# Position products of layer 0 from a table of distances, gathered through memory, in a two-layer attention kernel

## The chip, the cores and the metric

The kernel runs on one core of a Trainium2 chip. TensorE (PE) multiplies matrices into PSUM[...]; VectorE (DVE) and ScalarE (ACT) read PSUM and work in SBUF; GpSimd (POOL) and SyncE (SP) issue transfers here. The metric is the device time of one execution in microseconds. The kernel before takes 3813.87 us (median of three runs, 3813.14 to 3814.92).

## The reference

Two layers of attention over images of 32 x 32 tokens, 4 images, 768 channels, 12 heads of 64. Each layer adds its result to its input, after a group norm:

```python
x = x + _L0_conv_ref(_gn(x), ...)
x = x + _L1_conv_ref(_gn(x), ...)
```

Both layers add to the scores a bias of relative positions, computed from the query itself. For layer 0:

```python
attn = jnp.einsum('bqd,bkd->bqk', q, k) / np.sqrt(HD)
Rh = _get_rel_pos(h, h, rel_h)
Rw = _get_rel_pos(w, w, rel_w)
rel_bias_h = jnp.einsum('bhwc,hkc->bhwk', rq, Rh)
rel_bias_w = jnp.einsum('bhwc,wkc->bhwk', rq, Rw)
attn = attn.reshape(b * NH, h, w, h, w) + rel_bias_h[:, :, :, :, None] + rel_bias_w[:, :, :, None, :]
```

`Rh[h, k]` is row `h - k + 31` of a table of 63 rows: only the distance counts. So a query in image row h meets 32 neighbouring rows of the table, a window that moves with h; and the same for columns. Layer 1 does the same after a 3 x 3 depthwise convolution and a layer norm of q, k and v.

## The kernel before

**Pairs and stages.** Two heads are worked together as a pair: 64 channels each on 128 partitions. A stage is one image in one layer, six pairs (hp 0 to 5). The eight stages run in the order image 0 and 1 in layer 0, then both in layer 1, then images 2 and 3 likewise: 48 pairs, of which 0 to 11 and 24 to 35 are layer 0. While pair i is attended, pair i + 1 is prepared.

**Attention (`attend`).** For each of two chunks c of 512 queries and each of two groups g of four key blocks, PE computes four score blocks: two heads' q.k products (L820) and two products of the bias with a 0/1 matrix (L822). ACT takes the exponentials (L827). DVE sums them in layer 0 (L836, L838). PE multiplies with the values (L844, av). The sums of the last chunk are finished with a product z (L789) and four ACT instructions.

**Steps.** The loop yields four times for each group, twice behind the scores and twice behind av, so a pair has 16 steps. Scores are written just ahead of steps 0, 4, 8 and 12, av just ahead of 2, 6, 10 and 14. `Pair.plan` gives each piece of the preparation a step; `at` collects the pieces of a step in a list, and they are emitted in that order into each engine's queue. There is no scheduler: an engine works its queue strictly in order. Within a step, pieces of the group norm, of `mix_tokens` (L303) and of `mix_weights` (L290, L291) were put in the list ahead of those of the pairs, projections behind them.

**Layer 0 preparation.** Pair 0 and 1 compute q, k and v plainly. From pair 2 on (`in_sevens`), two pairs' products are made together by seven block products instead of eight (`sevens`): Q in two pieces at steps 0 and 2 (which make q and k of the pair), V at steps 8 and 10 for even hp only. So pairs with odd hp have few pieces. Pair 24 (`shift`) has all 4 steps later. For q, ACT writes the tile q and also q_t, the same with rows and columns exchanged (L495, L496).

**Position products (`positions`).** In two halves of 16 image rows and columns, PE multiplies for each row and head a 32-row window of the table with 32 queries: 64 products of 64 x 32 by 32 a half (L613), all into one bank. ACT copies them to the tile whole (L618 contiguous, L619 strided). In layer 0 pairs of the sevens the halves are at steps 6 and 8 (8 and 10 for pair 24).

**`split`** (step 10, or 12 for pair 24) casts whole to a rounded copy, high (L629, ACT), leaves the rest in whole (L630, DVE), and POOL issues the transfers that spread both into the two bias tiles (L640): 16 a pair, 8 for each chunk.

**PSUM.** Two banks are the first score tile's (ps_a), one av's, one small. The other four are two places, `place_b` and `place_c`, two banks each. A place is opened anew for each user: the second score block of each group takes both banks of place_b, the third both of place_c, and between them the preparation's products take singles of them. A new user waits until the old one has been read. The fourth score block uses ps_a again and waits for the first block's exponential.

**Transfers.** SP issues loads and stores in its own order; an issue that waits holds up those behind it. Weights are loaded two uses ahead.

## Time and profile before

| | |
|---|---|
| median of three runs | 3813.87 us |
| the profiled execution | 3816.61 us |
| its span, first to last instruction | 3814.6 us |
| granted TensorE clock | 0.997 |
| position products in PE, L613 | 123.6 + 122.7 us busy, both layers |
| q_t, L496 (ACT) | 48 + 22 + 22 + 4 instructions, 1.14 to 1.28 us |
| copies of positions, L618 and L619 (ACT) | 96 each, 54.9 and 99.9 us |
| cast to high, L629 (ACT) | 48, 49.9 us |
| rest in whole, L630 (DVE) | 48, 58.5 us |
| bias transfers, L640 (POOL) | 768, 2.9 and 3.0 us to landing |

A row of the groups names line, engine, operation, output and inputs, shape, count; then the time busy and the mean duration in ns; then the idle time of the engine ahead of it and what ended it. On PE each float32 product stands as two instructions, and successive products overlap, so a mean duration is longer than a product's share of the time; what a product costs is read from the starts in the timeline. A timeline row gives the start in us, the length of the merged row, engine, line, operation, tiles, shapes, count, and in brackets the idle time ahead of it with its releaser. From one start of scores to the next, a layer 0 pair with odd hp takes 55 us where nothing else is put beside it, and one with even hp some 74 us.

### The profile page before, as it was taken

The page shows a single profiled execution, that of the slowest core. Times are in us where ns is not written, and L with a number is a line of the kernel's source. Part 1 is how long each engine was busy: PE and PEld are TensorE (multiplying, and loading weights), DVE is VectorE, ACT ScalarE, POOL GpSimd, SP SyncE. Part 2 cuts the span into 40 slices and gives each one's busy share as a digit, 9 for nine tenths or more (in the row PEclk, how much of TensorE's full clock was granted, in tenths as well). Part 3 has the DMA queues.
Part 4 walks back from the last instruction along what each step waited for, and adds up shares of the span by engine and source line. Part 5 has one row for each costly group of instructions (what it writes and reads, how often), then busy time and mean ns, then how long its engine had stood idle before and what let it go on. Part 6 is the DMA issues. An engine that isn't in the chain of part 4 may idle for free. (4 is left out here: it accounts for less than half of the span.)

```text
span 3814.6 us, 76313 instructions
## 1 busy us (share of the span) xinstructions
PE 3749.5 (98%) x32990; PEld 1656.7 (43%) x32990; DVE 2467.1 (65%) x3068; ACT 1786.5 (47%) x2573; POOL 529.1 (14%) x964
## 2 busy tenths in 40 slices
PE   8999999999999999999999999999999999999998
PEld 4535535533344443444535445355343444434442
DVE  2566554559678877688454554445686888867874
ACT  2455434545355553455534544254442555525562
POOL 0111100111111211111200010001111112111120
PEclk9999999999999999999999999999999999999999
DMA  4344443331431223311333132523114212142123
GB/s 152 102 122 116 134 144 90 101 81 40 119 102 48 57 59 95 123 48 48 82 111 121 53 78 63 171 61 78 46 46 131 87 50 66 47 122 65 48 58 100
DMA packets 214024, 330.44 MB, mean 87 GB/s; under 512 B 50390, under 2 KB 103698, under 8 KB 213680
## 3 DMA queue, kind: packets, MB, share of 16 engines
q1 hardware_dynamic: 122912, 211.86, 17.9%
q0 software_dynamic: 90768, 113.61, 12.6%
q8 instruction: 263, 4.31, 0.5%
q14 instruction: 81, 0.66, 0.1%
HBM read 184.23 MB, written 40.10 MB: 59 GB/s over the span
## 5 line engine op out<-in xcount | busy, mean ns | idle before, releaser
L827 ACT ACTIVATE e<-s 128x1024 f32<-128x1024 f32 x768 | 775.6, 1024 | 423.7 <-PE s L822 393.6
L131 PE MATMUL qkv<-xn,wqkv_t 128*64 128x512 f32 x3648 | 816.0, 596 | 7.0 <-DVE gmean L334 2.6
L820 PE MATMUL s<-q,k 64*128 64x512 f32 x3072 | 808.7, 603 | 6.6 <-ACT e L827 3.1
L544 DVE SCALAR_TENSOR_TENSOR shared<-shared,sm 128x1056 f32<-128x1056 f32 x576 | 757.9, 1316 | 15.7
L822 PE MATMUL s<-bias,ones 64*128 64x512 f32 x1536 | 611.7, 790 | 1.1 <-DMA bias<-whole 1.0
L844 PE MATMUL av<-e,vt 128*64 128x512 f32 x2624 | 596.2, 596 | 0.0
L131 PEld LDWEIGHTS qkv<-xn,wqkv_t 128*64 128x64 f32 x3648 | 256.5, 137 | 484.0 <-issue 466.1
L640 POOL DMA_DIRECT2D bias<-high x384 | 205.6, 556 | 1794.6 <-ACT high L629 1559.7
L838 DVE TENSOR_TENSOR acc<-acc,e 128x1024 f32<-128x1024 f32 x294 | 360.0, 1225 | 114.0 <-ACT e L827 87.4
L820 PEld LDWEIGHTS s<-q,k 64*128 64x128 f32 x3072 | 279.5, 186 | 264.4 <-issue 213.3
L527 ACT ACTIVATE shared<-qkv,sm 128x512 f32<-128x512 f32 (+1 forms) x288 | 129.3, 502 | 469.7 <-PE qkv L131 469.7
L844 PEld LDWEIGHTS av<-e,vt 128*64 128x64 f32 x2624 | 185.4, 137 | 350.9 <-issue 316.8
L822 PEld LDWEIGHTS s<-bias,ones 64*128 64x128 f32 x1536 | 148.6, 187 | 185.4 <-issue 184.1
L640 POOL DMA_DIRECT2D bias<-whole x384 | 207.2, 571 | 53.2 <-DVE whole L630 46.3
L836 DVE TENSOR_TENSOR acc<-e 128x1024 f32<-128x1024 f32 x49 | 60.0, 1225 | 215.4 <-ACT e L827 206.8
L742 ACT COPY weighed<-av 128x512 f32<-128x512 f32 x96 | 56.3, 587 | 279.0 <-PE av L844 270.1
L559 DVE TENSOR_REDUCE mean<-ln_c 128x8 f32<-128x512 f32 x144 | 98.6, 685 | 106.0 <-PE ln_c L556 106.0
L771 POOL DMA_DIRECT2D weighed<-last x94 | 50.7, 541 | 679.6 <-ACT last L768 638.6
L613 PEld LDWEIGHTS rel<-q,rel 64*32 64x32 f32 x6144 | 112.1, 106 | 68.6 <-issue 63.8
L613 PE MATMUL rel<-q_t,rel 64*32 64x32 f32 x6144 | 123.6, 195 | 1.8 <-issue 1.8
L613 PE MATMUL rel<-q,rel 64*32 64x32 f32 x6144 | 122.7, 195 | 1.9 <-issue 1.9
L412 DVE TENSOR_TENSOR shared<-shared,m3m 128x512 f32<-128x512 f32 x66 | 45.3, 687 | 119.9 <-PE m3m L131 119.8
(162 smaller groups left out, 4439.0 us busy)
## 6 DMA issues: line engine op xcount, KB each, us to landing
bias<-high POOLq DMA_DIRECT2D x384, 128.0 KB, 2.9
bias<-whole POOLq DMA_DIRECT2D x384, 128.0 KB, 3.0
wqkv_t<-in_wqkv SPq DMA_DIRECT2D x78, 384.0 KB, 3.2
wqkv_t<-mixed SPq DMA_DIRECT2D x66, 384.0 KB, 3.1
wproj_t<-mixed SPq DMA_DIRECT2D x48, 384.0 KB, 3.3
wqkv_t<-in_wqkv SPq DMA_DIRECT2D x66, 192.0 KB, 2.5
xn<-in_x SPq DMA_DIRECT2D x24, 512.0 KB, 7.7
x<-in_x SPq DMA_DIRECT2D x48, 256.0 KB, 3.2
```

What stands on the lines that cost most here:

```text
L131: nc.tensor.matmul(ps[lo : lo + D], a[:, lo : lo + D], b, start=start, stop=stop, **kw)
L527: nc.scalar.activation(self.pad[s][:, rows, there : there + src.shape[2]], src, AF.Identity, bias=col(self.column(s)))
L544: nc.vector.scalar_tensor_tensor(y, window, tap, y, ALU.mult, ALU.add)
L559: nc.vector.tensor_reduce(of, heads, AX.X, ALU.add)
L613: nc.tensor.matmul(ps[lo : lo + S, k * S : (k + 1) * S].rearrange("p (b c) -> p b c", b=2), rel[rows, 2 * self.layer + i, first : first + ...
L640: nc.gpsimd.dma_start(sets, some.unsqueeze(1).to_broadcast([D // 2, 2, QC]))
L820: nc.tensor.matmul(ps[:, j, :], k[rows, keys], q[rows, cols], start=True, stop=False)
L822: nc.tensor.matmul(ps[:, j, :], ones[rows, kt % 2 * P : (kt % 2 + 1) * P], bias[c][rows, kt // 2, :], start=False, stop=True,)
L827: nc.scalar.activation(e, ps, AF.Exp)
L836: nc.vector.tensor_tensor(acc, es[0], es[1], ALU.add)
L838: nc.vector.tensor_tensor(acc, acc, e, ALU.add)
L844: nc.tensor.matmul(av[j * D : (j + 1) * D, :], pair.vt[:, kt, j * D : (j + 1) * D], e[:, j, :], start=(kt == 0), stop=(kt == NKT - 1),)
```

## The change

Pairs 1 to 11 and 24 to 35 no longer use `positions`. A block of queries that spans 16 image rows and 16 columns needs 47 neighbouring rows of the table, for all its queries together. `all_positions` multiplies all 64 channels with such a table: a stationary matrix of 64 x 128 holds 47 distances for rows and 47 for columns, for each combination of row half and column half (four in all). A call takes half of the queries, in two products of 256 queries for each head. The first head's result goes to one bank (rel0), read by ACT, the second's to another (rel1), read by DVE. Each is copied in two parts, one contiguous in runs of 16 and one strided, to tiles that take the buffers of q_t and whole.

Each query's result is now 47 distances from which 32 are wanted, at an offset that depends on its row or column. `keep_positions` stores both heads' results to memory (two stores of 512 KB), and `call_positions` reads them back with eight transfers, in which each image row (or column) starts one partition's row further on: runs of 64 elements, 256 bytes. `split` then reads them from the tile raw in four ACT copies and four DVE subtractions of 64 x 512 instead of one of each.

The calls are at steps 3 (in place_c) and 4 (in place_b), store and gather at 6, split at the head of step 9 (pair 24: 7, 8, 10, and the head of 12). Halves of steps place a piece at the head of its step's list. q_t is made only where `positions` is still used: pair 0 and layer 1. The table's rows are no longer reversed, so windows, the 0/1 matrix (picks) and split's row choice are reversed to match; their cost is unchanged. The table is loaded once at the start.

```diff
+            self.by_table = not self.layer and self.i > 0
+            self.all = []
...
-                self.q_t = one.tile([P, T], F32, tag="q_t", name="q_t")
+                if not self.by_table:
+                    self.q_t = one.tile([P, T], F32, tag="q_t", name="q_t")
             nc.scalar.activation(self.q[:, cols], ps, AF.Identity, bias=bias, scale=scale)
+            if self.by_table:
+                return
...
+        def all_positions(self, b, place):
+            if not self.all:
+                self.all = [one.tile([P, T], F32, tag=tag, name="all_" + tag) for tag in ("q_t", "whole")]
+            place.n = 0
+            ps = [place.single(f"rel{j}") for j in range(2)]
+            for a in range(2):
+                tokens = slice(b * HALF + a * (HALF // 2), b * HALF + (a + 1) * (HALF // 2))
+                there = slice(a * (HALF // 2), (a + 1) * (HALF // 2))
+                for j in range(2):
+                    rows = slice(j * D, (j + 1) * D)
+                    nc.tensor.matmul(
+                        ps[j][:, there], table[rows, 2 * a + b, :], self.q[rows, tokens], start=True, stop=True
+                    )
+            for j, (to, copy) in enumerate(zip(self.all, (nc.scalar.copy, nc.vector.tensor_copy))):
+                copy(by_rows(to[:D], b), ps[j][:D].rearrange("p (s m c) -> p s m c", s=2, m=S // 2))
+                copy(by_columns(to[D:])[:, b], ps[j][D:].rearrange("p (a c) -> p a c", a=S))
+            if place is place_b:
+                other_work((place_c, place_c, place_b, place_b))
+
+        def keep_positions(self):
+            self.kept = dram.tile([P, 2, T], F32, tag="kept", name="kept", bufs=2)
+            for j, x in enumerate(self.all):
+                nc.sync.dma_start(self.kept[:, j, :], x)
+
+        def call_positions(self):
+            self.raw = one.tile([P, T], F32, tag="q_t", name="raw")
+            kept = self.kept[:, :, :]
+            step = 2 * T
+            for i in range(2):
+                for j in range(2):
+                    for h in range(2):
+                        first = i * D + j * S + h
+                        nc.sync.dma_start(
+                            self.raw[first : first + S - 1 : 2, :].rearrange("p (m x) -> p m x", m=S // 2),
+                            bass.AP(
+                                kept.tensor, kept.offset + (i * D + h * (S // 2)) * step + j * T,
+                                [[step, S // 2], [step + 2 * S, S // 2], [1, 2 * S]],
+                            ),
+                        )
...
-            nc.scalar.copy(high, self.whole)
-            nc.vector.tensor_tensor(self.whole, self.whole, high.bitcast(F32), ALU.subtract)
+            if self.by_table:
+                self.whole = one.tile([P, T], F32, tag="whole", name="low")
+                for b in range(2):
+                    cols = slice(b * HALF, (b + 1) * HALF)
+                    views = [
+                        (x[:D, cols].rearrange("p (s m c) -> p s m c", s=2, m=S // 2) for x in (high, self.whole)),
+                        (x[D:, cols].rearrange("p (a c) -> p a c", a=S) for x in (high, self.whole)),
+                    ]
+                    for (to, left), x in zip(views, (by_rows(self.raw[:D], b), by_columns(self.raw[D:])[:, b])):
+                        nc.scalar.copy(to, x)
+                        nc.vector.tensor_tensor(left, x, to.bitcast(F32), ALU.subtract)
+            else:
+                nc.scalar.copy(high, self.whole)
+                nc.vector.tensor_tensor(self.whole, self.whole, high.bitcast(F32), ALU.subtract)
...
-                first = 4 if shift(self.i) else 6
                 pieces += [
-                    (first, lambda: self.positions(0)),
-                    (first + 2, lambda: self.positions(1)),
-                    (first + 4, lambda: self.split()),
+                    (3, lambda: self.all_positions(1, place_c)),
+                    (4, lambda: self.all_positions(0, place_b)),
+                    (6, lambda: self.keep_positions()),
+                    (6, lambda: self.call_positions()),
+                    (8.5 if shift(self.i) else 9.5, lambda: self.split()),
                 ]
...
-        events.setdefault(step, []).append(piece)
+        events.setdefault(int(step), []).insert(0 if step % 1 else len(events.get(int(step), [])), piece)
...
+    at(-8, lambda: [nc.sync.dma_start(table[rows], tables[0]) for rows in (slice(0, D), slice(D, P))])
```

More of the change, by code (lines that the diff above doesn't have):

```diff
@@ L45, in two_layers @@
 @with_exitstack
-def two_layers(ctx: ExitStack, tc: tile.TileContext, keep, x_in, wqkv, wproj, rels, windows, vrow, small, const, onehot, picks, out):
+def two_layers(ctx: ExitStack, tc: tile.TileContext, keep, x_in, wqkv, wproj, rels, windows, tables, vrow, small, const, onehot, picks, out):
     nc = tc.nc
@@ L131, in halves, with by_rows, by_columns @@
             nc.tensor.matmul(ps[lo : lo + D], a[:, lo : lo + D], b, start=start, stop=stop, **kw)
+    def by_rows(x, b):
+        return x.rearrange("p (m s b c) -> p b s m c", m=S // 2, s=2, b=2)[:, b]
+    def by_columns(x):
+        return x.rearrange("p (c b a) -> p b a c", b=2, a=S)
     def image(x):
@@ L371, in two_layers @@
     seen = fixed.tile([P, 2 * len(items) * (T // QC)], F32, tag="seen", name="seen")
+    table = fixed.tile([P, 4, P], F32, tag="table", name="table")
     tiny = fixed.tile([P, 1], F32, tag="tiny", name="tiny")
@@ L611, in positions @@
                         lo = i * D + j * S
-                        first = 2 * (S - 1 - at)
+                        first = 2 * at
                         nc.tensor.matmul(
@@ L638, in split @@
                             sets = bias[2 + part :: 4, 2 * h : 2 * h + 2, :] if i else bias[part::4, h::2, :]
-                            some = src[i * D + h : (i + 1) * D : 2, cols]
+                            some = src[i * D + 1 - h : (i + 1) * D : 2, cols]
                             nc.gpsimd.dma_start(sets, some.unsqueeze(1).to_broadcast([D // 2, 2, QC]))
@@ L649, in plan @@
                     (2, lambda: self.plain(Q, 1)),
-                    (4, lambda: self.plain(K, 0)),
+                ] + ([
+                    (3, lambda: self.all_positions(0, place_c)),
+                    (4, lambda: self.all_positions(1, place_b)),
+                    (6, lambda: self.keep_positions()),
+                    (6, lambda: self.call_positions()),
+                    (9, lambda: self.split()),
+                ] if self.by_table else [
                     (5, lambda: self.positions(0)),
-                    (6, lambda: self.plain(K, 1)),
                     (7, lambda: self.positions(1)),
                     (8, lambda: self.split()),
+                ]) + [
+                    (4, lambda: self.plain(K, 0)),
+                    (6, lambda: self.plain(K, 1)),
                     (8, lambda: self.plain_v(0)),
@@ L662, in plan @@
                 ]
-                first = 4 if shift(self.i) else 6
                 pieces += [
-                    (first, lambda: self.positions(0)),
-                    (first + 2, lambda: self.positions(1)),
-                    (first + 4, lambda: self.split()),
+                    (3, lambda: self.all_positions(1, place_c)),
+                    (4, lambda: self.all_positions(0, place_b)),
+                    (6, lambda: self.keep_positions()),
+                    (6, lambda: self.call_positions()),
+                    (8.5 if shift(self.i) else 9.5, lambda: self.split()),
                 ]
@@ L1073, in general @@
 @with_exitstack
-def general(ctx: ExitStack, tc: tile.TileContext, bad, x_in, wqkv, wproj, rels, windows, vrow, small, const, onehot, picks, out):
+def general(ctx: ExitStack, tc: tile.TileContext, bad, x_in, wqkv, wproj, rels, windows, tables, vrow, small, const, onehot, picks, out):
     nc = tc.nc
@@ L1328, in _laid_out @@
     onehot = np.concatenate([np.arange(S)[:, None] == key // S, np.arange(S)[:, None] == key % S])
-    windows = np.stack([rels[..., h : h + 3 * S // 2 - 1] for h in (0, S // 2)], axis=-1)
+    rows = rels[..., ::-1]
+    windows = np.stack([rows[..., h : h + 3 * S // 2 - 1] for h in (0, S // 2)], axis=-1)
+    tables = np.zeros((2, D, 2, 2, 2, D), np.float32)
+    for i in range(2):
+        for half in range(2):
+            some = rows[i::2, :, half * (S // 2) : half * (S // 2) + 3 * S // 2 - 1]
+            which = (half, slice(None), 0) if i == 0 else (slice(None), half, 1)
+            tables[(slice(None), slice(None)) + which + (slice(0, some.shape[-1]),)] = some[:, :, None]
     picks = np.zeros((S // 2, 2, 2, 2, 2, 2, 8, S // 2), np.float32)
@@ L1334, in _laid_out @@
         for u in range(2):
-            picks[i, 0, :, :, :, u] = (8 * u + np.arange(8) == i)[:, None]
-        picks[i, 1, ..., i] = 1.0
+            picks[i, 0, :, :, :, u] = (8 * u + np.arange(8) == S // 2 - 1 - i)[:, None]
+        picks[i, 1, ..., S // 2 - 1 - i] = 1.0
     return {
@@ L1342, in _laid_out @@
         "windows": np.ascontiguousarray(windows.reshape(4, D, 3 * S - 2)),
+        "tables": np.ascontiguousarray(tables.reshape(2, D, 4, P)),
         "vrow": np.ascontiguousarray(f["L0_conv_bv"].reshape(1, C)),
```

## The prediction

> **What bounds the kernel now.** I read the page's busy shares first, then the groups of lines, then the timeline of one pair of layer 0, engine by engine.

> ```profile
> span 3814.6 us, 76313 instructions
> PE 3749.5 (98%) x32990; PEld 1656.7 (43%) x32990; DVE 2467.1 (65%) x3068; ACT 1786.5 (47%) x2573; POOL 529.1 (14%) x964
> ...
> L827 ACT ACTIVATE e<-s 128x1024 f32<-128x1024 f32 x768 | 775.6, 1024 | 423.7 <-PE s L822 393.6
> ...
> L618 ACT COPY whole<-rel 64x512 f32<-64x512 f32 x96 | 54.9, 572 | 28.3 <-PE rel L613 28.3
> ```

> TensorE is busy for 98%, so PE work removed is time won, and any wait put before PE is time lost: there are only 65 us of idle PE to hide in. The other two engines have room on average, but ACT waits for scores and PE for the exponentials' banks, so order counts. Pair 27, prepared while pair 26 is attended (2087.7 to 2142.9 us), on PE:

> ```profile
> 2119.27 3.65 PE L844 MATMUL av<-e,vt 128*64 128x512 f32 x16
> 2122.86 0.21 PE L613 MATMUL rel<-q,rel 64*32 64x32 f32 x1
> ...
> 2124.08 1.13 PE L820 MATMUL s<-q,k 64*128 64x512 f32 x4
> ...
> 2128.63 1.08 PE L789 MATMUL z<-acc,cst 128*64 128x512 f32 x4
> ...
> 2130.86 3.65 PE L844 MATMUL av<-e,vt 128*64 128x512 f32 x16
> 2134.44 1.13 PE L820 MATMUL s<-q,k 64*128 64x512 f32 x4
> ```

> Position products take 2122.86 to 2124.08, 1.22 us, and again between z and av: z to av is 2.23 us, of which z alone is 0.91 (2092.25 to 2093.16 earlier), leaving 1.3. And ACT there, then DVE in the attention of pair 4:

> ```profile
> 2129.75 0.60 ACT L790 ACTIVATE t<-z 128x512 f32<-128x512 f32 x1
> ...
> 2133.53 1.04 ACT L629 CAST high<-whole 128x1024 fp32r<-128x1024 f32 x1
> 2135.84 4.29 ACT L827 ACTIVATE e<-s 128x1024 f32<-128x1024 f32 x4 [1.26 <-PE s L822]
> ```

> ```profile
> 355.31 5.21 DVE L838 TENSOR_TENSOR acc<-acc,e 128x1024 f32<-128x1024 f32 x4 [1.70 <-ACT e L827]
> 360.44 1.75 DVE L303 TENSOR_TENSOR shared<-xn 128x1536 f32<-128x1536 f32 x1
> ```

> ACT has just 1.26 us of slack between the split's cast and the next exponentials. On DVE the token mixing runs at once behind the sums of exponentials.

> [...] two heads' q.k products plus two bias products take 1.09 us a block (2125.27 to 2126.36 on the same view), which 512-column passes of 0.43 us allow only if both heads overlap. [...] for ACT writes: L619, strided, 1041 ns against L618's 572. For DVE, and for strided reads, it shows nothing. [...]

> **The change, part by part.** A pass of 512 columns is 2.58/6 = 0.43 us (m4m, 12 instructions in two column groups, 2093.16 to 2095.74). Position products removed: 1.22 + 1.3 = 2.5 us a pair. Added: per call two halves of 256 columns, two passes each, heads side by side: 4 x 0.215 = 0.86, 1.72 a pair. [...] PE gain 0.8 us a pair, 23 pairs: **-18.4**.

> ACT loses q_t (2 x 1.17) and four L618/L619 copies (3.2) and one cast (1.04), and gains four rel0 copies (3.2) and four split copies (3.2): even, but elsewhere. DVE gains four copies from PSUM (0.69 each by L559's row) and four subtractions of 64x512 for one of 128x1024 (1.22): +4.3 us a pair, hidden by idle time except as below.

> *Third score block.* The first call, after the second sevens, holds place_c until ACT has copied rel0. ACT's k copy ends 2116.28; two copies 0.58 + 1.04 make 2117.9. PE, after 0.86 more and two blocks of 1.09, comes at 2117.86. With signal latency a wait of 0.15, 22 pairs: **+3.3**. Behind it the exponentials start 1.7 us later; they still end before av needs them.

> *Late DVE copies.* Where another piece stands ahead of rel1's copies on DVE, the score block that wants their bank waits. Pairs 5 and 29 (mix_tokens' pieces come first in step 4): sums of e end 2124.1 on pair 27's clock, then 2 x 1.75, then 2 x 0.69: 2129.0, against PE at 2125.9: 3.1 each. Pairs 6 and 10 (weight mixing, 5 x 0.55 us, ahead in step 3): rel1 at 2119.7 against 2117.9: 1.8 each. Together **+9.8**.

> *The round trip.* On pair 27's clock rel1's copies end at 2125.6. Two stores of 512 KB follow: the 256 KB store mid<-x lands in 3.1 us, and another 256 KB takes 0.7 to 0.9, so 3.9: 2129.6. SP then issues eight gathers. wproj_t<-in_wproj (384 runs of 512 B) takes 0.38 to issue, so about 0.45 apart: the eighth at 2132.9; landing like a 192 KB load's 2.3: 2135.2. Everything on SP behind these waits too, but the next weight loads are half a pair away. ACT cannot go past its first split copy: of the four (0.58, 1.04, 0.58, 1.04) the second needs the last gathers, so they end at 2137.9 and the next exponential at 2138.9. (Strided reads are not in the trace: 0.58 to 1.04 a copy; I take the strided write's 1.04, and at 0.58 the stall is 0.9 shorter.) PE has by then run av and three score blocks and wants that bank at 2137.3 (its clock, less 0.8): **1.8 to 2 us of stall**. Behind ACT here stand the exponentials, behind those av; the bias DMAs on POOL also start later, but land at about 2143.5, before the next pair's bias product at about 2144.7.

> Pairs with an even hp have V's first sevens (10.5 us of PE) at step 8, pairs 7, 25 and 31 a projection, 11 and 35 padded products: covered. Pair 1 is covered by plain K and V, pair 24 by V. Exposed: 3, 5, 9, 27, 29, 33 (the four of 55.2 us or so from start to start, and the like). Pairs 9, 27, 33: 2.0 each, **+6**. Pairs 5, 29: 1.8 each more, **+3.6**. Pair 3: weight mixing at step 6 has five stores ahead on SP, behind DVE's statistics (2.46) and mixing (2.66): the stores of positions start 5.8 us later: **+8**. Were the cover of the even pairs gone, each would pay the same 2 us.

> *Removed waits.* Two waits of next pair's bias (1.0 and 0.4 us) go, since the split's program place is earlier: **-1.4**. The table's load (two DMAs) is at the start, long before use: nothing. The picks and reversed rows change data only.

> Sum: -18.4 + 3.3 + 9.8 + 6 + 3.6 + 8 - 1.4 = **+10.9 us**. The profiled execution took 3816.6 us (span 3814.6, 2.0 around it), 2.7 over the median; on the median, 3813.9 + 11 = 3825.

> **Rivals.** *Hidden round trip (not slower).* If the gathers land by 2133.5, that is 7.8 us from rel1's copies instead of 9.6, ACT meets no wait. For: small stores land in 2.0 at the least, and the DMA engines are nearly idle there. Against: medians. Pairs 9, 27, 33, 5, 29 then cost no ACT stall and pair 3 costs 6: -18.4 + 3.3 + 9.8 + 6 - 1.4 = -0.7, so 3813. It decides from a trip of about 7.8 us down; to be clearly faster, PE must win over 1.1 us a pair too.

> *Strided DVE copies are as dear as ACT's.* Then rel1's second copy is 1.1, not 0.69: place_b is late by 0.3 for the second block of step 8 in some 18 pairs (+5.4), and the trip starts 0.4 later in six (+2.4): 3833. For: L619. Against: no DVE row shows it. Bounds: 0.69 to 1.3 a copy; I take 0.69.

> *The heads do not overlap.* A call takes 1.72 us, a pair 3.44: +0.9 instead of -0.8, 39 us worse: 3864. Against: q.k in the same form does overlap. Best for PE would be 1.0 won a pair: 3820.

> *Gathers are slow.* 256-byte runs: packets of 512 B took 28 ns and 376 B 29 in the trace; 2048 of 256 B over 16 engines at some 20 ns are 2.6 us, beneath the issue time. If issue is 0.75 (rel<-in_windows at start, behind a full queue, took 0.73), 2.1 later in six pairs: 3838.

> **How the numbers follow.** Forecast 0.42; hidden trip 0.25; strided DVE 0.18; slow gathers 0.11; no overlap 0.04. Within 0.2% (7.6 us) is about what measurement can tell from no change, so same is 3806.2 to 3821.5. The hidden trip's 0.25 is split 0.14 same, 0.11 faster (PE winning more); of the forecast 0.09 falls below 3821.5 if the trip is 1 us shorter: slower 0.66, same 0.23, faster 0.11. Range 3807 to 3842: it leaves out the lowest faster end and the no-overlap case. The forecast's own range is 3817 to 3832.

> **What would show it.** Right: the table's products take 0.86 us a call; PE idles some 2 us before the fourth score block of step 12 in pairs 9, 27 and 33, released by an exponential that followed a split copy waiting for raw's DMA; some 3 us before the second block of step 8 in pairs 5 and 29, released by DVE; layer 1's pairs keep their lengths. Wrong: gathers landing under 8 us after the copies, calls longer than 1 us, or PE waits in the even pairs.

## The result and the profile after

The changed kernel takes 3867.96 us (median of four runs, 3861.42 to 3868.77) against 3814.39 us for the kernel before on the same chip: a ratio of 1.0137, with a 95% interval of 1.0119 to 1.0154. It is slower by 53.6 us where 10.9 were forecast. The page of its profiled execution:

```profile
span 3867.0 us, 66034 instructions
PE 3754.1 (97%) x27470; PEld 1641.7 (42%) x27470; DVE 2602.3 (67%) x3229; ACT 1789.7 (46%) x2596; POOL 524.9 (14%) x964
...
L908 ACT ACTIVATE e<-s 128x1024 f32<-128x1024 f32 x768 | 772.3, 1026 | 431.3 <-PE s L903 402.9
```

PE carries out 5520 instructions fewer and is nevertheless busy 4.6 us longer. The page alone does not explain that; the table below does, with 10.4 us less of work and 15.4 us more lost at half clock. In the changed kernel's numbering the scores are L901 and L903, av L925, the table's products L651, their copies L655 (contiguous) and L656 (strided), the gathers L676, the high copies L698 and the low subtractions L699. The names m1m and m4m stand for block products of the sevens, p1p and p4p for those of the projection.

Pair 27 again, prepared while pair 26 is attended, on PE and then on ACT:

```profile
2154.09 1.13 PE L651 MATMUL rel<-q,table 64*128 64x256 f32 x8
2155.06 1.02 PE L901 MATMUL s<-q,k 64*128 64x512 f32 x4
...
2159.51 1.02 PE L651 MATMUL rel<-q,table 64*128 64x256 f32 x8
2160.46 3.65 PE L925 MATMUL av<-e,vt 128*64 128x512 f32 x16
...
2178.10 1.13 PE L901 MATMUL s<-q,k 64*128 64x512 f32 x4 [1.26 <-ACT e L908]
```

```profile
2172.09 0.60 ACT L698 CAST high<-raw 64x512 fp32r<-64x512 f32 x1
2174.17 2.83 ACT L698 CAST high<-raw 64x512 fp32r<-64x512 f32 x3 [1.48 <-DMA raw<-kept]
2177.02 3.77 ACT L908 ACTIVATE e<-s 128x1024 f32<-128x1024 f32 x4
```

A call takes PE 0.97 and 0.95 us. ACT waits 1.48 us for the gather, the exponentials behind it start late, and PE waits 1.26 us for their bank. This is the round trip as forecast: rel1's copies end at 2165.24, ACT goes on at 2174.17, 8.9 us later (9.6 forecast).

The late copies of head 1 show in attend 4, behind mix_tokens' pieces on DVE, and the clock behind them: the four instructions of a score block's q.k take 1.96 us, where pair 27's above take 1.13.

```profile
373.18 0.68 DVE L655 COPY all_whole<-rel 64x512 f32<-64x512 f32 x1
373.87 1.02 DVE L656 COPY all_whole<-rel 64x512 f32<-64x512 f32 x1
...
375.04 1.96 PE L901 MATMUL s<-q,k 64*128 64x512 f32 x4 [3.39 <-DVE all_whole L656]
```

Here is where the time lies. An attend runs from its first score to the next pair's; "short" attends are those that prepare pairs 3, 5, 9, 27, 29 and 33; "with V" are those in which V is made for a pair with even hp (pair 24 apart). Idle is the time in which no PE instruction runs. "Half clock" is half of the busy time that falls in stretches where the record of the clock shows 0.5. The rest is what PE's work takes at full clock. All are differences between the two profiled spans, in us:

| attends | forecast | measured | idle PE | half clock | rest |
|---|---|---|---|---|---|
| short: 2, 4, 8, 26, 28, 32 | +19.9 | +22.5 | +17.0 | +7.3 | -1.8 |
| beside a projection: 6, 24, 30 | -2.0 | +22.5 | +15.5 | +9.3 | -2.3 |
| with V: 1, 3, 5, 7, 9, 25, 27, 29, 31, 33 | -3.0 | +7.5 | +11.0 | +1.7 | -5.2 |
| others | -4.0 | -0.3 | +3.7 | -2.9 | -1.1 |
| sum | +10.9 | +52.2 | +47.1 | +15.4 | -10.4 |

The forecasts follow from the prediction's terms: 23 pairs at -18.4 + 3.3, that is -0.66 each, and its waits where it put them. Each row is computed apart, so the last digits of sums may differ by 0.1; another 0.2 us lies ahead of the first attend. The -2.9 in "others" lies in layer 1, which keeps the old products: there the kernel before had three stretches at half clock, in attends 22, 46 and 47, and the changed kernel has two.

Three costs that no term of the sum has show in attend 6. Two are on DVE. Before, the projection's sums (L902 there) and its addition (L923) come directly behind the sums of exponentials:

```profile
487.41 2.55 DVE L838 TENSOR_TENSOR acc<-acc,e 128x1024 f32<-128x1024 f32 x2
489.88 5.50 DVE L902 TENSOR_TENSOR os_sums<-q 128x512 f32<-128x512 f32 x9
...
509.44 2.55 DVE L838 TENSOR_TENSOR acc<-acc,e 128x1024 f32<-128x1024 f32 x2
511.99 0.69 DVE L923 TENSOR_TENSOR os_sums<-os_sums,p1p 128x512 f32<-128x512 f32 x1
```

After:

```profile
508.64 0.68 DVE L655 COPY all_whole<-rel 64x512 f32<-64x512 f32 x1
509.34 1.02 DVE L656 COPY all_whole<-rel 64x512 f32<-64x512 f32 x1
510.39 5.51 DVE L983 TENSOR_TENSOR os_sums<-q 128x512 f32<-128x512 f32 x9
...
532.93 3.53 DVE L699 TENSOR_TENSOR low<-raw,high 64x512 f32<-64x512 f32 x4
536.49 0.69 DVE L1004 TENSOR_TENSOR os_sums<-os_sums,p1p 128x512 f32<-128x512 f32 x1
```

The projection's sums (L983) now stand behind rel1's copies, and PE starts p4p 1.97 us late. Its addition L1004 stands behind 3.53 us of low subtractions, and p1p waits for it. The list of waits from 505 to 540 us has both (total, times, longest, in us):

```profile
PE p1p L131 <- DVE os_sums L1004: 3.1, 1, 3.1
...
PE p4p L131 <- DVE os_sums L983: 2.0, 1, 2.0
```

The attends with V pay in the same way. In attend 5 the low subtractions, at the head of their step, push back weight mixing and with it the addition L423, for which m1m waits:

```profile
453.01 2.87 DVE L699 TENSOR_TENSOR low<-raw,high 64x512 f32<-64x512 f32 x3 [0.43 <-ACT high L698]
...
460.57 0.68 DVE L423 TENSOR_TENSOR shared<-shared,m1m 128x512 f32<-128x512 f32 x1
461.30 1.97 PE L131 MATMUL m1m<-wqkv_t,shared 128*64 128x128 f32 x32 [2.63 <-DVE shared L423]
```

The third cost is the clock. Busy time by stretch around the p4p wait of attend 6: the columns are the stretch, its length, the busy time of PE, PEld, DVE, ACT and POOL with instructions, then the granted TensorE clock, and last what DMA moved.

```profile
508.50:511.20 2.70, 0.76 (x4) 0.00 (x0) 2.62 (x5) 0.59 (x1) 0.00 (x0) 1.00 0.48 194
511.70:515.10 3.40, 3.40 (x11) 1.15 (x9) 3.40 (x6) 0.00 (x0) 0.00 (x0) 0.51 0.53 148
515.10:534.00 18.90, 18.90 (x92) 7.24 (x88) 12.43 (x18) 9.48 (x14) 1.84 (x4) 1.00 0.39 113
```

Behind this wait the clock is halved for 3.4 us, and 1.97 us of idle time cost 3.7. Half-clock stretches, without the one in which each execution ends, sum to 51.2 us in the changed kernel and to 17.1 before.

### The profile page after: what moved, and what is told of

Its sections match the earlier page's. It is cut to its first block, busy times and chain, and to the rows that moved or that the text cites. A ratio compares the mean times of both kernels' runs of the same rounds, so it can differ in the third digit from the quotient of the medians.

```text
span 3867.0 us, 66034 instructions
## 1 busy us (share of the span) xinstructions
PE 3754.1 (97%) x27470; PEld 1641.7 (42%) x27470; DVE 2602.3 (67%) x3229; ACT 1789.7 (46%) x2596; POOL 524.9 (14%) x964
## 4 chain that ended last, share of the span: by engine, by line
PE 43%; DVE 5%; ACT 2%; DMA 1%; issue 1%; SPq 0%; ACTq 0%; DVEq 0%; POOLq 0%
PE qkv L131 9%; PE s L901 8%; PE av L925 7%; PE m4m L131 2%; PE m3m L131 2%; PE p4p L131 2%; PE m1m L131 2%; PE p3p L131 2%; PE s L903 2%; PE p1p L131 1%; PE m L131 1%; DVE shared L558 1%; DVE acc L919 1%; PE ln_c L570 1%; PE rel L627 1%
## 5 line engine op out<-in xcount | busy, mean ns | idle before, releaser
L901 PE MATMUL s<-q,k 64*128 64x512 f32 x3072 | 817.0, 607 | 28.7 <-ACT e L908 17.3
L903 PE MATMUL s<-bias,ones 64*128 64x512 f32 x1536 | 619.4, 797 | 0.0
L925 PE MATMUL av<-e,vt 128*64 128x512 f32 x2624 | 597.0, 597 | 0.0
L901 PEld LDWEIGHTS s<-q,k 64*128 64x128 f32 x3072 | 281.4, 187 | 295.8 <-issue 206.7
L925 PEld LDWEIGHTS av<-e,vt 128*64 128x64 f32 x2624 | 185.5, 137 | 355.0 <-issue 324.1
L903 PEld LDWEIGHTS s<-bias,ones 64*128 64x128 f32 x1536 | 151.5, 188 | 182.0 <-issue 181.3
L131 PE MATMUL m4m<-xn,wqkv_t 128*64 128x512 f32 x528 | 120.9, 592 | 1.0 <-ACT t L871 1.0
L131 PE MATMUL m1m<-shared,wqkv_t 128*64 128x512 f32 x528 | 120.9, 592 | 0.5 <-ACT last L849 0.5
L131 PE MATMUL m3m<-xn,wqkv_t 128*64 128x512 f32 x528 | 120.8, 592 | 0.0
L584 DVE TENSOR_REDUCE lnv<-shared 128x16 f32<-128x1024 f32 x72 | 87.5, 1216 | 48.0 <-ACT shared L580 48.0
L423 DVE TENSOR_TENSOR shared<-shared,m3m 128x512 f32<-128x512 f32 x66 | 45.4, 687 | 103.3 <-PE m3m L131 103.2
```

The source lines that it names most:

```text
L131: nc.tensor.matmul(ps[lo : lo + D], a[:, lo : lo + D], b, start=start, stop=stop, **kw)
L584: nc.vector.tensor_reduce(v, squared.rearrange("p (a d) -> p a d", d=D), AX.X, ALU.add)
L901: nc.tensor.matmul(ps[:, j, :], k[rows, keys], q[rows, cols], start=True, stop=False)
L903: nc.tensor.matmul(ps[:, j, :], ones[rows, kt % 2 * P : (kt % 2 + 1) * P], bias[c][rows, kt // 2, :], start=False, stop=True,)
L925: nc.tensor.matmul(av[j * D : (j + 1) * D, :], pair.vt[:, kt, j * D : (j + 1) * D], e[:, j, :], start=(kt == 0), stop=(kt == NKT - 1),)
```

## The experiments

All medians are compared with the kernel before, run on the same chips (medians 3815.2 to 3816.2 us); "below the changed kernel" is against 3868.0.

**The pairs beside a projection take the old products.**

```diff
-            self.by_table = not self.layer and self.i > 0
+            self.by_table = not self.layer and self.i > 0 and self.i not in (7, 25, 31)
```

The plan of those three pairs keeps its old steps for the old products.

> Pairs 7, 25 and 31 (prepared while a projection runs) go back to the old position products; the other 20 pairs keep the table. Theory A, VectorE's queue: the copies of head 1 stand ahead of the projection's sums and the low subtractions ahead of its additions, and this makes up the 5.9, 10.6 and 5.9 us by which attends 6, 24 and 30 grew: about 22 us less than the changed kernel, 3845 us, and no TensorE gap ahead of p4p or p1p in these attends. Theory B, the trip through memory as the prediction had it: these three pairs are covered and each gained 0.65 us, so 2 us more than the changed kernel, 3870 us.

Measured: 3848.7 us, ratio 1.0087 (1.0070 to 1.0104), 19 us below the changed kernel. Attends 6, 24 and 30 are again within 0.01 us of the kernel before, and no gap stands ahead of p4p or p1p in them. This is theory A's result for these three, as far as taking out all of the table's pieces can show it; the next experiment and the fourth say which piece holds up which product. Elsewhere a new gap (m4m in attend 23, 3.5 instead of 1.7 us) takes back 3 us.

**The low subtractions later.**

```diff
-                    (8.5 if shift(self.i) else 9.5, lambda: self.split()),
+                    (8.5 if shift(self.i) else 9.5, lambda: self.split("high")),
+                    (10 if shift(self.i) else 11, lambda: self.split("low")),
```

"high" issues ACT's four copies, "low" the four subtractions and the bias transfers; plain pairs likewise at 9 and 11.

> In all 23 table pairs the four low subtractions on VectorE, and the bias transfers behind them, are issued 2 steps later (1.5 where the split was at a half step); ScalarE's four high copies stay where they are. Theory A, VectorE's queue: the subtractions no longer hold the additions that release m1m (1.5 to 2.6 us in attends 3, 5, 9, 27, 33, together 8.6 us) and p1p (3.1 us in attends 6, 24, 30, together 9.2 us), and half-clock stretches behind them go too: 18 to 22 us less than the changed kernel, 3846 to 3850 us. Theory B, the trip through memory: what is late is the gather that ScalarE's copies wait for, which stays where it is: no change, 3867 us.

Measured: 3852.5 us, ratio 1.0094 (1.0077 to 1.0111), 15.5 below. All five m1m gaps and all three p1p gaps are gone, and the attends with V go from 7.5 us above the kernel before to 4.6 below it. So theory A holds, in its place as well as in its sign. It falls 2.5 us short of the smaller figure; moving the same piece for pair 24 made its bias late: PE waits 7.56 us for a bias transfer at 1923.7 us, which is in the total.

**No trip through memory.**

```diff
-                nc.sync.dma_start(self.kept[:, j, :], x)
+                pass
...
-            self.raw = one.tile([P, T], F32, tag="q_t", name="raw")
+            self.raw = self.all[0]
+            return
```

> Leaves out the store to memory and the eight gathers in the 23 table pairs: the split reads head 0's copied bank directly, so the position terms added to the scores are not those of their keys. Theory B, the trip through memory: with no gather to wait for, pairs 3, 5, 9, 27, 29 and 33 come down by the 17.6 us charged to the trip, and the waits ahead of p1p and m1m go too if ScalarE's copies were late because of the gathers: 3830 us or below. Theory A, VectorE's queue: only the three gaps that end with the gather go (5.4, 2.6 and 1.3 us, with 10 us at half clock behind them worth about 5): 14 us less, 3853 us, and the gaps ahead of p4p (2.0, 3.6, 2.0), p1p (3.1 each) and m1m (1.5 to 2.6) stay.

Measured: 3858.7 us, ratio 1.0112 (1.0095 to 1.0129), 9 below. Attends 2, 8, 26 and 32 now end 0.4 us below the kernel before: what they had lost was the trip, 14.5 us with their gains. Attends 4 and 28 stay 6.0 and 4.7 us above, and the gaps ahead of p4p, p1p and m1m stay at 1.9 to 3.6, 3.1 and 1.5 to 2.6 us. Theory A, then, for most of the time, and the trip as forecast for four of the short attends. The attends with V lose 5.7 us more. The trace has that as four new waits of 1.3 to 1.5 us in attends 3, 9, 27 and 33, where PE's product z waits for DVE's copy of the group norm's mean (L342). In attend 3 this copy stands behind 3.52 us of low subtractions and 5.21 us of sums of exponentials. In the kernels below that move the subtractions none of the four waits is there.

**Head 1's copies on ScalarE.**

```diff
-            for j, (to, copy) in enumerate(zip(self.all, (nc.scalar.copy, nc.vector.tensor_copy))):
+            for j, (to, copy) in enumerate(zip(self.all, (nc.scalar.copy, nc.scalar.copy))):
```

> Head 1's four copies per pair (1.7 us for two) go from VectorE to ScalarE behind head 0's; nothing else changes. Theory A, VectorE's queue: the gaps at pairs 5 and 29 that end with VectorE's strided copy (3.4 us each) and those ahead of p4p (2.0, 3.6 and 2.0 us) go, with five half-clock stretches behind them worth about 10 us: up to 24 us less than the changed kernel, less what ScalarE's exponentials lose by 3.4 us more copying in each of 23 pairs; 3845 to 3860 us. Theory B, the trip through memory: VectorE's copies are not what is late, and ScalarE's longer queue can only delay the store: 3867 to 3877 us.

Measured: 3881.5 us, ratio 1.0176 (1.0159 to 1.0193), 13.5 above the changed kernel: both theories missed. The gaps that theory A named did go (those of 3.4 us at pairs 5 and 29, and all three ahead of p4p). But 22 new ones of 1.42 to 1.46 us stand ahead of a third score block, as here in attend 28:

```profile
2292.46 0.56 ACT L655 COPY all_q_t<-rel 64x512 f32<-64x512 f32 x1
2293.04 1.03 ACT L656 COPY all_q_t<-rel 64x512 f32<-64x512 f32 x1
...
2294.67 1.01 ACT L656 COPY all_whole<-rel 64x512 f32<-64x512 f32 x1
...
2295.73 1.13 PE L901 MATMUL s<-q,k 64*128 64x512 f32 x4 [1.42 <-ACT all_whole L656]
```

The bank of the first call is released by the last of four copies instead of by the last of two in each engine. So two readers are worth their place: with one the change costs more.

**The table's pieces ahead of the mixing.** In each step the pair's products, copies, store and gathers (wrapped so that they bear the name table_piece) are put at the head of the list.

```diff
-            at((i - 1) * n_steps + r, piece)
+            at((i - 1) * n_steps + r, piece, pair.by_table and piece.__name__ == "table_piece")
```

> Only the order within a step changes: the table's products, its copies, the store and the gathers of a pair are issued ahead of the weight mixing and the group norm of the same step, on every engine. Theory A, queues (VectorE's and SyncE's): the gaps behind the strided copy (3.4 us at pairs 5 and 29, 1.9 us in attends 5 and 9) and those behind the gather (5.4, 2.6 and 1.3 us) go, 20 us, with about 10 us of half-clock loss behind them: 3837 to 3848 us; the gaps ahead of p4p, p1p and m1m stay. Theory B, the trip itself is too long: the gathers move up by no more than the mixing's own issues, so pairs 3, 9, 27 and 33 keep about 2 us each and only pairs 5 and 29 recover: 3858 us or above.

Measured: 3858.2 us, ratio 1.0109 (1.0094 to 1.0125), 10 below: theory B's number, though not all its places, since attends 4 and 28 did not recover. The short attends fall from 22.5 to 16.6 us above. The 3.4 us gaps behind VectorE's copy are gone, but gaps of 2.0 to 2.5 us stand in attends 2, 4, 8 and 28; in attend 8 ACT's high copy waits 2.7 us for the gather. With the queue cleared, the gather comes to light behind it.

**Ahead, and no trip.** Both edits together.

> All 23 table pairs, issued ahead of the mixing as in the kernel that only changed this order, and with the store and the gathers left out, so that the position terms added are not those of their keys. Theory B: the six short attends (2, 4, 8, 26, 28, 32) all end 0.4 us below the kernel before, where the order alone left 3.4, 3.5, 3.9, 1.5, 3.7 and 0.6 us above it. Theory A: attends 4 and 28 stay 3 us or more above, since their copies and not the gather are late. Both: p4p, p1p and m1m keep their gaps, about 3840 us in all.

Measured, in one run: 3852.9 us. Five of the six short attends (2, 8, 26, 28, 32) end 0.4 us below the kernel before, so in these the gather was what was left. Attend 4 stays 3.4 above, with neither a gather nor a late copy. The list of waits there, 370 to 378 us:

```profile
ACT e L915 <- DVE acc L924: 2.2, 1, 2.2
PE s L908 <- ACT e L915: 2.0, 1, 2.0
```

The token mixing, pushed behind rel1's copies, now holds up the sums of exponentials. It seems that DVE has more work in that attend than fits, in whatever order; the combined kernel below shows the same place with ten mixing instructions between rel1's copies (end 363.8 us) and the sum (375.0 us). The total was missed by 13 us, through the attends with V: they end 13.4 us above the kernel before, where the order alone left 6.6, and the four waits of z behind the group norm's mean are back.

**Combined, with 19 and with 13 table pairs.** Ahead, low later, and the old products in some pairs.

```diff
-            self.by_table = not self.layer and self.i > 0
+            self.by_table = not self.layer and self.i > 0 and self.i not in (7, 24, 25, 31)
```

And with 13, the even pairs:

```diff
-            self.by_table = not self.layer and self.i > 0
+            self.by_table = not self.layer and self.i > 0 and self.i in (1, 2, 4, 6, 8, 10, 11, 26, 28, 30, 32, 34, 35)
```

> Pairs 7, 24, 25 and 31 take the old position products; the other 19 keep the table, issued ahead of the mixing, with the low subtractions 2 steps later. Theory A: nothing waits any more, and each of the 19 pairs gains the 0.5 us of TensorE that undisturbed pairs show: 3805 us, at most 3815. Theory B, the table's trip leaves a wait of 2 us or more in each of the six pairs whose attends are short: 3820 us or above.

> As the combined kernel, but the six pairs with short attends (3, 5, 9, 27, 29, 33) take the old position products too: 13 pairs with the table. Theory A: 13 times 0.5 us below the kernel before: 3808 us, and 2 to 3 us above the combined kernel. Theory B: 3808 us too, but more than 10 us below the combined kernel.

Measured: combined 3822.9 us, ratio 1.0020 (1.0013 to 1.0027); even pairs 3811.1 us, ratio 0.9987 (0.9981 to 0.9994). The first comes out where theory B put it: its six short attends stay 0.6 to 4.0 us above the kernel before, 10.8 together. But a wait of about 2 us, as theory B had it in each of the six, is there only in attends 2, 4 and 32 (1.7, 2.0 and 2.7 us). The second is 4 us faster than the kernel before, and the only one here that is: in it the attends with V end 5.9 us below the kernel before and the short ones 0.04 above. Both theories had 3808 us for it, 3 us less. That is the change's worth where little waits.

**The split later in the short attends.** Against the combined kernel:

```diff
-                    (8.5 if shift(self.i) else 9.5, lambda: self.split("high")),
-                    (10 if shift(self.i) else 11, lambda: self.split("low")),
+                    (9.5 if self.hp % 2 == 0 else 11.5, lambda: self.split("high")),
+                    (11 if self.hp % 2 == 0 else 12, lambda: self.split("low")),
```

> The combined kernel (19 table pairs), but in the pairs without V products the high copies are issued 2 steps later and the low subtractions 1 step later, so that the gathers have some 7 us more to land before ScalarE needs them. Theory B (in the short attends what is left is the gather, which ScalarE's copies wait for ahead of the exponentials): the waits of 1.4 to 2.7 us in attends 2, 4, 8, 28 and 32 go and each of these attends ends 0.4 us below the kernel before: 3805 us, below the even-pairs kernel. Theory A (what is left is a queue and not the gather) or a bias that is now late for the next pair: no better than the combined kernel, 3820 us or above.

Measured: 3863.4 us, ratio 1.0128 (1.0111 to 1.0145), 40 us worse than the combined kernel. Two things were wrong in the expectation. ACT's copies did not move: between the exponentials of the third and the fourth score group it has nothing else than the split and the finish of z, so steps 9.5 and 11.5 are one place in its queue, and the wait for the gather stayed (2.0 us in attend 2, 1.9 in the combined kernel). The subtractions did move, and the bias became late for the next pair:

```profile
387.08 1.13 PE L921 MATMUL s<-q,k 64*128 64x512 f32 x4
395.46 0.80 PE L923 MATMUL s<-bias,ones 64*128 64x512 f32 x2 [7.25 <-DMA bias<-low]
```

So neither place tried in a short attend is free: before the fourth group's exponentials the gather is not there yet, and one step later the bias misses its deadline.

**Pauses of a known length.** The kernel before, with extra ACT work that makes PE pause in layer 1.

```diff
+                    if c == 0 and kt == 4 and pair.i % 24 in range(13, 23):
+                        for _ in range(pair.i % 24 - 9):
+                            nc.scalar.copy(idle, idle)
```

> The kernel before, with 4 to 13 extra ScalarE copies of an unused tile (128x512, some 0.5 us each) ahead of the first exponential of steps 4 in 20 attends of layer 1 (4 in attends 13 and 37, one more in each following one), so that TensorE pauses for different times. Theory C, the clock: a pause that takes at least about 1.9 us out of one 3.41 us window of the clock's record is followed by a 3.41 us window at half clock, and that attend grows by its pause plus 1.7 us; a pause that is shorter or lies across two windows costs only itself. Rival: the half clock in the record changes no time, and each attend grows by its pause alone.

Measured, in one run: 3883.1 us. What counts here are single attends. Attends 18 and 42 do the same work and get the same nine copies, and PE pauses 3.11 us in both. Two stretches of each, the pause and the 6 us behind it, with the columns as above:

```profile
1442.00:1445.10 3.10, 0.00 (x1) 0.00 (x0) 3.00 (x5) 3.00 (x6) 0.00 (x0) 0.86 0.00 0
1445.10:1451.08 5.98, 5.96 (x16) 1.91 (x18) 5.84 (x6) 2.82 (x3) 0.00 (x0) 0.50 0.00 1
3364.50:3367.70 3.20, 0.09 (x4) 0.03 (x2) 3.10 (x5) 3.10 (x6) 0.00 (x0) 1.00 0.00 0
3367.70:3373.70 6.00, 6.00 (x28) 2.09 (x30) 5.86 (x6) 2.66 (x3) 0.00 (x0) 1.00 0.00 0
```

Behind the first the clock is 0.50 and PE carries out 16 instructions in 6 us, behind the second 1.00 and 28. Attend 18 grew by 5.43 us, attend 42 by 2.56 (their idle time by 2.5 in both). A window here is one step of the grid of 3.413 us on which the record's stretches at half clock start. The second pause lies across two windows, 1.40 us in one and 1.71 in the next; the first took 2.25 us out of one. With 1.81 us of pause, attends 16 and 40 grew by 2.1 and 2.3 and kept the full clock; with 2.46 us, attends 17 and 41 grew by 5.8 and 4.4, behind 6.8 and 3.4 us at half clock. Theory C holds in these six attends as to where half clock came, and the rival, by which the record has no effect on time, does not. Theory C's 1.7 us on top is right for attend 41 (1.7 us lost at half clock); in attends 17 and 18, where half clock lasted two windows, 3.2 and 3.0 us were lost.

## Why the prediction was wrong

The sign was right: waits put before PE cost more than the PE work that the change removes. The time was outside the range. By its own steps:

Of the rivals, the hidden round trip is refuted by ACT's 1.48 us wait for raw. "Strided DVE copies are as dear as ACT's" is true (L656 takes 1.02 to 1.11 us on DVE against 0.68 for L655), but it isn't what decided. The heads do overlap: a call takes 0.96 us, not 1.72. Gathers issue 0.65 us apart (0.45 forecast), as the slow-gather rival half assumed; the trip was still shorter than forecast, for two reasons. Two of the eight gathers read only the first head's store and went ahead of the second's landing (issued at 2165.76 and 2166.36); the forecast had all eight behind it. And the second store landed sooner: the first gather behind it is issued 2.85 us after it (2165.27 to 2168.12), where 3.9 were taken, the author's estimate from the 3.1 us of a 256 KB store. Packets of 256 B took 17.7 ns in the mean, where "some 20" was an estimate too.

## What to carry to other kernels

The engines did their queues in order here (in attend 6 the addition L1004 stood behind 3.53 us of low subtractions), so ask of each added instruction not whether the engine has idle time, but which instruction behind it another engine waits for, in every stage that differs: a projection beside the same pieces turned a gain into 22 us of loss. Add the clock to the price of a wait on a nearly saturated TensorE: here a pause of 3.11 us made attend 42 2.56 us longer at full clock, and attend 18 5.43 us, with half clock behind it. And a change that gains half a microsecond in some pairs and loses several in others can be applied to the first alone; here, with the order of its pieces changed too, that was 4 us faster than the kernel before.

## What was not expected of the hardware

That half clock follows waits as short as these was not expected: the prediction charged no wait for it. In the traces of before and after, idle PE time was counted in each window of the 3.413 us grid that ran at full clock. Half clock followed 16 of these 2215 windows, with 1.87 to 3.25 us idle; the others had 1.87 us at most. The two sides meet there to within 0.01 us, with PE's ends being modelled and some records missing. Of the 20 windows at half clock, 16, with at most 0.21 us idle, were followed by full clock, and four, with 0.89 us or more, by another at half clock. In attend 18 of the pauses the first window at half clock had 0.86 us idle; a second one followed, and 3.0 us were lost instead of 1.7. The pause of 3.11 us in attend 42, 1.40 and 1.71 us in two windows, cost nothing extra. Whether such differences are why four runs of the changed kernel spread over 7 us was not tested.
